# Layer 1 of a fused conv and state-space kernel: ACT scales the normalised tokens and sums the batch statistics, PE turns them back, DVE takes a second block of delta times x

## The chip, the cores and the metric

The kernel runs on one core of one Trainium2 chip. The metric is device time in microseconds (us) of one execution; the time before is the median of three runs. The engines are named as in the profile: PE (matmuls; PEld is its weight load), DVE (the vector engine), ACT (the scalar engine), POOL (GpSimd) and SP (the queue that issues the DMAs). Each engine works through its own instructions in the order in which the program emits them, and semaphores make it wait for the others.

## What is computed

The input x is 32 images of 96 channels, 56 x 56. Two stages follow each other. The first (an inverted bottleneck with squeeze and excitation) is not touched by the change. The second is, for each image, two state-space layers over the 3136 tokens, then a 1x1 convolution with a pooled branch, a batch normalisation over all images, and a residual:

```python
for i in range(2):                                     # seq: (32, 3136, 96)
    h = (seq - mean) * rsqrt(var + 1e-5) * ln_g + ln_b # over the 96 channels
    xs, z = split(h @ in_w)                            # 192 channels each
    xc = silu(causal_conv4(xs) + conv_b)
    dt, Bm, Cm = split(xc @ xproj_w)                   # 6, 16, 16
    delta = softplus(dt @ dt_w + dt_b)
    hs = scan(exp(delta * A), delta * Bm * xc)         # 192 channels x 16 states
    y = (sum over states of hs * Cm + Dp * xc) * silu(z)
    seq = seq + y @ out_w
out = fus_w @ concat(seq, relu(mean(x) @ gp_w + gp_b)) + fus_b
out = (out - mean(out)) * rsqrt(var(out) + 1e-5) * bn_g + bn_b + x   # over images and pixels
```

## The kernel before

Everything is float32. The first stage fills the first 3.5 ms or so and writes `x1d` to DRAM. The last 0.4 ms normalise `pred` and add the residual. The 15.2 ms in between are the two state-space layers.

**Units.** An image is cut into four chunks of 784 tokens (`LC`), and a chunk in one layer is a unit. There are 256 units; the list alternates a layer 0 unit of one chunk with a layer 1 unit of an older chunk. The state of the scan is carried from chunk to chunk in `state`.

**Steps.** A unit is 24 steps (`NT`), each a scan over 128 rows, 8 channels with 16 states. A block `k` of 64 channels takes 8 steps: 4 groups of states `j`, 2 halves `p`. One loop over `at` emits everything by hand. In step `at` it emits, in this order:

```python
inject(at + 4)   # POOL: bx = u * B, for the two halves at once         L851
decay(at + 1)    # ACT: da = exp(delta * A), into PSUM, two buffers     L831
bring(at)        # ACT: cp = copy of C into PSUM, one buffer, odd steps L839
early[at]        # the three Silu and Softplus, each with two table loads L587, L588
gated(at - 6); scan(at); product(at - 1)  # DVE: z *= y L914; scan L863; hc = hh * cp L871
save(at - 2); rest(at); reduce(at - 5)    # ACT L886; POOL hc L878; PE y L898, L903
todo[at]         # the rest, below; then the DMAs that fetch later steps
```

**The rest** is spread over steps by two lists. `prepare(n)` makes the inputs of unit n while the two units before it are scanned: its step t comes out in step t mod 24 of a unit. `finish(n)` projects the result one unit later. Within one step, `todo` holds the steps of the younger unit (small t) ahead of those of the older one (t over 23). What matters here, by step of the running unit:

- Steps 4 to 7, `finish`: PE makes the two halves `o` (L769, L773); ACT stores half 0 in step 6 and half 1 in step 7 (`seq` L779 for layer 0, `pre` L783 for layer 1, in the same buffer as `sq`). Step 19: DVE takes `bn_stats` of the two halves of a layer 1 unit (L788), and SP writes them to `pred`.
- Steps 23, 0, 1 and 2, younger unit: PE centers the tokens (`cen`), ACT copies the centered halves to `xm` (L618) and squares them (L619); the root follows.
- Steps 8 and 9: PE spreads the reciprocal roots over the channels, `rstd` (L656). Step 11: DVE multiplies both halves, `xn = xm * rstd` (L663).
- Step 12 and 13: PE runs the convolution of block 0, `xs`, from `xn` (`conv`, L675); step 14: ACT copies it to `xc` (`keep`, L686). Blocks 1 and 2 follow in steps 14 and 16, the copies in 16 and 18. Step 19 (early): Silu of `xc`.
- Step 11 (early), older unit: Softplus of `dl` on ACT, then `delta` is written to DRAM, and POOL makes blocks 1 and 2 of `us = dl * xc` (L725). Step 12: ACT copies block 0 of `xc` to PSUM (`up`, L730), DVE makes block 0 of `us` (L733), and SP writes `us` to DRAM in two DMAs; `fetch` reads it back for the next unit from step 16 on.

**Banks.** All these PE results, and `up`, take turns in two PSUM buffers: `bank()` (line 463) gives the n-th result the buffer of the n-2nd, so its first writer waits for that one's last reader.

Of the kernel before, what the change touches and what calls it, by code (L numbers as in the profile page):

```python
# [11 lines left out]
F32 = mybir.dt.float32  # L12
AF = mybir.ActivationFunctionType
ALU = mybir.AluOpType
AX = mybir.AxisListType
# [4 lines left out]
B, C, H, W = 32, 96, 56, 56  # L20
L = H * W
# [3 lines left out]
NL, NS, DIN, RANK, KC = 2, 16, 192, 6, 4  # L25
LC = 784
HB = LC // 2
LP = 512
NQ = L // LC
# [4 lines left out]
NB = DIN // 64  # L34
NT = 2 * NB * SG
TK = 112
NK = LC // TK
# [16 lines left out]
def conv_mamba_kernel(ctx, tc, a, out):  # L54
    nc = tc.nc
    v, s, g, pe, sp = nc.vector, nc.scalar, nc.gpsimd, nc.tensor, nc.sync

    const = ctx.enter_context(tc.tile_pool(name="const", bufs=1))
# [16 lines left out]
    gpw = load("gpw", [C, C])  # L75
    fusw = load("fusw", [C, 2, C])
    g2 = const.tile([C, B], F32, name="g2", tag="g2")
    stats = const.tile([C, B * NQ * 2, 6], F32, name="stats", tag="stats")

    def bn_fold(pool, gam, bet, mean, var, p, n, name):  # L80

# [13 lines left out]
    with ExitStack() as ph:  # L95
# [102 lines left out]
        for i in range(NHB):  # L198
            t = hp3.tile([128, H + 2, W + 2], F32, name=f"hpad{i}", tag=f"hpad{i}")
# [248 lines left out]
    with ExitStack() as ph:  # L448
# [5 lines left out]
        udram = ph.enter_context(tc.tile_pool(name="l1u", bufs=3, space=DRAM))  # L454
# [42 lines left out]
        ps = bank("acol")  # L497
# [16 lines left out]
        for i in range(NL):  # L514
            v.tensor_copy(lnb[:, i, C : C + 1], cp[:, LNB + i : LNB + i + 1])
            ps = bank(f"lnb_{i}")
# [43 lines left out]
        for k in range(NB):  # L560
            ps = bank(f"wf_{k}")
# [5 lines left out]
        state = [wts.tile([128, NT], F32, name=f"state{i}", tag=f"state{i}") for i in range(NL)]  # L567

        xn = wts.tile([C + 1, KC - 1 + LC], F32, name="xn", tag="xn")
# [4 lines left out]
        work = ph.enter_context(tc.tile_pool(name="l1", bufs=1))  # L574
        MAIN = "natural_log_exp_and_others"
        nch = B * NQ

        units = [(0, 0), (1, 0)]
        for c in range(2, nch):
# [3 lines left out]
        seqs = {}  # L583

        def through(t, func):

            s.activation(t, t, func)  # L587
            s.preload_act_table_set(MAIN)  # L588
# [3 lines left out]
        def cols(h):  # L592
            return slice(h * HB, h * HB + HB)

        def prepare(n):
# [5 lines left out]
            c, i = units[n]  # L601
            b, q = divmod(c, NQ)
            d = data[n]
# [9 lines left out]

            def square(h):
                if h == 0:
                    d["xm"] = wt([C, LC], "xm", 1, n)
                    d["sq"] = wt([C, LC], "sq", 1, n)
                s.copy(d["xm"][:, cols(h)], d["cen", h][:C, :HB])  # L618
                s.activation(d["sq"][:, cols(h)], d["cen", h][:C, :HB], AF.Square)  # L619

            def variance():
# [26 lines left out]
                    if q == 0:  # L648
                        g.memset(xn[:, : KC - 1], 0.0)

            def spread_root(h):
                ps = d["rstd", h] = bank(f"rstd_{n}_{h}")
                for k in range(NK):
                    lo, hi = max(k * TK, h * HB), min((k + 1) * TK, h * HB + HB)
                    if lo < hi:
                        pe.matmul(  # L656
                            ps[:C, lo - h * HB : hi - h * HB], d["rs"][:, k : k + 1].to_broadcast([TK, C]),
                            eye[:TK, lo - k * TK : hi - k * TK], start=True, stop=True,
                        )

            def normalise(h):
                to = xn[:C, KC - 1 + h * HB : KC - 1 + h * HB + HB]
                v.tensor_mul(to, d["xm"][:, cols(h)], d["rstd", h][:C, :HB])  # L663

            def trail():
                if q + 1 < NQ:
# [44 lines left out]
                for r in both:  # L711
                    pe.matmul(ps[r, :HB], wd[r, i, k, :], d["bcs"][r, :], start=True, stop=True)

            def spread(tag, t):
                to = d[tag] = udram.tile([DIN, LC], F32, name=f"{tag}d_{n}", tag=f"{tag}d")
                for h in range(2):
                    sp.dma_start(to[:, cols(h)].rearrange("(k m) l -> m k l", k=NB), t[h * 64 : h * 64 + 64])

            def softplus():
                through(d["dl"], AF.Softplus)  # L720
                spread("delta", d["dl"])

            def input_u():
                d["us"] = wt([128, NB, HB], "us", 1, n)
                g.tensor_mul(d["us"][:, 1:], d["dl"][:, 1:], d["xc"][:, 1:])  # L725

            def bring_x():

                d["up"] = bank(f"up_{n}")
                s.copy(d["up"][:, :HB], d["xc"][:, 0])  # L730

            def input_u0():
                v.tensor_mul(d["us"][:, 0], d["dl"][:, 0], d["up"][:, :HB])  # L733
                spread("u", d["us"])


            late, then = (9, 4) if n in (3, len(units) - 1) else (0, 0)
            steps = [(-4, load)]
# [1 line left out]
                steps += [(-1 + h + late, lambda h=h: center(h)), (-1 + 1 + h + late, lambda h=h: square(h))]  # L740
            steps += [(-1 + 2 + late, variance), (-1 + 3 + late, root), *[(t + late, lambda m=m: newton(m)) for m, t in enumerate((2, 2, 3))]]
            for h in range(2):
                steps += [(8 + h + then, lambda h=h: spread_root(h)), (11 + then, lambda h=h: normalise(h))]
            steps += [(11 + 3 + then, trail)]
            for k in range(NB):
                t = (12, 14, 16)[k] + then
# [3 lines left out]
            for k in range(NB):  # L750
                steps += [((17, 19, 21)[k] + then, lambda k=k: gate(k)), ((18, 20, 22)[k] + then, lambda k=k: keep("z", 3, "zp", k))]
                steps += [((22, 22, 23)[k] + then, lambda k=k: project_dt(k)), ((23, 23, 24)[k] + then, lambda k=k: keep("dl", 1, "dtp", k))]
            steps += [(26.5 + then, lambda: through(d["z"], AF.Silu)), (34.5 + then, softplus), (35 + then, input_u)]
            steps += [(36 + then, bring_x), (36 + then, input_u0)]
            return steps

        def finish(n):

            c, i = units[n]
            b, q = divmod(c, NQ)  # L760
            d = data[n]
# [12 lines left out]

            def store(h):
                if i + 1 < NL:
                    if h == 0:
                        seqs[c, i + 1] = wt([C, LC], f"seq{i + 1}", 3, n)
                    s.copy(seqs[c, i + 1][:, cols(h)], d["o", h][:C, :HB])  # L779
                    return  # L780
                if h == 0:
                    d["pre"] = wt([C, LC], "sq", 1, n)
                s.activation(d["pre"][:, cols(h)], d["o", h][:C, :HB], AF.Identity, bias=g2[:, b : b + 1])  # L783

            def count():
                if i + 1 == NL:
                    for h in range(2):
                        v.bn_stats(stats[:, 2 * c + h, :], d["pre"][:, cols(h)])  # L788
                    sp.dma_start(pred[b][:, q * LC : (q + 1) * LC], d["pre"])
                data[n] = {}  # L790

            return [
                (4, lambda: [project(k) for k in (None, 0, 1)]), (5, lambda: project(2)),
                (6, lambda: store(0)), (7, lambda: store(1)), (19, count),
            ]

        LAG = 5

        def place(t):
            k, r = divmod(t, 2 * SG)  # L800
            return k, r // 2, r % 2
# [76 lines left out]
                g.tensor_mul(hcs[at - 1][:, :, LP:], hhs[at - 1][:, :, LP:], beside(data[n]["C", j][:, LP:]))  # L878

        def save(at):  # L880
            n, t = divmod(at, NT)
            c, i = units[n]
            p = place(t)[2]
            hh = hhs[at - p] if p == 0 else hhs.pop(at - p)
            if c % NQ + 1 < NQ:
                s.copy(state[i][:, t : t + 1], hh[:, p, LC - 1 :])  # L886

        def reduce(at):

# [63 lines left out]
    with ExitStack() as ph:  # L953
        last = ph.enter_context(tc.tile_pool(name="last", bufs=3))
        one = ph.enter_context(tc.tile_pool(name="last1", bufs=1))
        mv = one.tile([C, 2], F32, name="mv", tag="mv")
        v.bn_aggr(mv, stats.rearrange("p n k -> p (n k)"))
        inv, sh = bn_fold(one, cp[:, BNG : BNG + 1], cp[:, BNB : BNB + 1], mv[:, 0:1], mv[:, 1:2], C, 1, "bn")
        for b in range(B):
            pre = last.tile([C, L], F32, name=f"lp{b}", tag="lp")  # L960
            res = last.tile([C, L], F32, name=f"lr{b}", tag="lr")
            sp.dma_start(pre, pred[b])
            sp.dma_start(res, x1d[b])
            s.activation(pre, pre, AF.Identity, bias=sh, scale=inv)
            v.tensor_add(res, res, pre)
            sp.dma_start(out[b], res)
# [61 lines left out]
```

## Time and profile before

| | |
|---|---|
| median of 3 runs | 19243.92 us (19236.5 to 19254.51) |
| the profiled execution | 19246.5 us, span 19243.6 us |
| the state-space layers, 3460 to 18700 us of the span | 15240 us, 59.5 us for each of 256 units |
| busy in that stretch: DVE, POOL, ACT, PE | 14955.52, 15124.08, 12552.34, 11335.55 us |
| mean granted clock of PE in that stretch | 0.79 of full speed |
| mean of one scan with a state, one `hc` on DVE, one `bx` on POOL, one `da` on ACT | 1835, 1194, 3573, 917 ns |

A line of the timeline gives the start from the beginning of the span, the duration, the engine, the line of the program, the operation with output and inputs, how many were merged, and in brackets how long the engine had been idle before it and what ended that. The duration of an instruction overlaps the start of the next one on its engine a little, so sums are better made from starts. The waits view gives, for each pair of waiting line and releasing line, the total in us, the times, and the longest.

### The profile page before, as it was taken

How to read it: one execution, taken by the hardware profiler on the slowest of the kernel's cores; microseconds unless marked ns; L12 is line 12 of the kernel's file. 1: busy time of each engine (PE TensorE's matmuls, PEld its weight loads, DVE VectorE, ACT ScalarE, POOL GpSimd, SP SyncE). 2: the span in 40 equal slices, each digit the busy share in tenths (PEclk: the TensorE clock that was granted, in tenths of full speed). 3: DMA queues.
4: the chain of work that ended last, by engine and by line, in shares of the span. 5: the costliest groups of instructions: out<-in, count | busy, mean ns of one | idle time of the engine just before them, and what ended most of it. 6: DMA issues, size and time to landing. Idle time of an engine off the chain costs nothing.

```text
span 19243.6 us, 282933 instructions
## 1 busy us (share of the span) xinstructions
PE 14489.7 (75%) x105692; PEld 5827.2 (30%) x105692; DVE 18041.5 (94%) x13684; ACT 14174.9 (74%) x23979; POOL 15509.9 (81%) x6606
## 2 busy tenths in 40 slices
PE   7999999677777777777777777777777777777760
PEld 3544444222222222222222222222222222222220
DVE  7888888699999999999999999999999999999993
ACT  3444444688888888888888888888888888888872
POOL 0000000699999999999999999999999999999991
PEclk9999999787777777877787778777877777778875
DMA  1000000355555555555555555555555555555548
GB/s 27 23 26 27 22 26 22 117 163 164 161 161 164 162 161 162 163 163 164 163 163 161 164 163 161 161 163 163 161 161 163 163 164 162 163 162 164 162 159 246
DMA packets 1049037, 2679.90 MB, mean 139 GB/s; under 512 B 129592, under 2 KB 342928, under 8 KB 1035368
## 3 DMA queue, kind: packets, MB, share of 16 engines
q1 hardware_dynamic: 1047656, 2661.80, 43.9%
q8 instruction: 828, 13.57, 0.3%
q14 instruction: 553, 4.53, 0.1%
HBM read 2211.05 MB, written 449.58 MB: 138 GB/s over the span
## 4 chain that ended last, share of the span: by engine, by line
DVE 35%; issue 24%; ACT 22%; PE 12%; POOL 4%; DMA 2%; SPq 1%; DVEq 0%; POOLq 0%; ACTq 0%
DVE hh L863 18%; DVE hc L871 12%; ACT da L831 5%; ACT L587 4%; ACT L588 3%; PE dw L276 3%; PE c L374 3%; POOL bx L851 2%; ACT cp L839 2%; DVE h L302 2%; DMA lr<-x1d 2%; PE bc L700 1%; PE c L223 1%; ACT dl L587 1%; ACT z L587 1%
## 5 line engine op out<-in xcount | busy, mean ns | idle before, releaser
L851 POOL TENSOR_TENSOR bx<-ub,B 128x1568 f32<-128x1568 f32 x3072 | 10975.8, 3573 | 25.2 <-DMA ub<-ud 15.8
L863 DVE TENSOR_TENSOR_SCAN hh<-da,state,bx 128x784 f32<-128x784 f32 x4608 | 8307.1, 1835 | 50.4 <-ACT da L831 44.8
L831 ACT ACTIVATE da<-deltab,acol 128x784 f32<-128x784 f32 x6144 | 5631.3, 917 | 2158.3 <-DVE hh L863 2124.2
L878 POOL TENSOR_TENSOR hc<-hh,C 128x544 f32<-128x544 f32 x3072 | 4210.3, 1371 | 40.2 <-DVE hh L863 28.8
L675 PE MATMUL xs<-xn,wx 97*64 97x392 f32 x12288 | 2907.0, 610 | 1356.5 <-DVE xn L663 1355.9
L871 DVE TENSOR_TENSOR hc<-hh,cp 128x1024 f32<-128x1024 f32 x3072 | 3667.7, 1194 | 0.1
L903 PE MATMUL y<-hc,rel 128*32 128x392 f32 x24576 | 3016.7, 579 | 367.7 <-DVE hc L871 349.2
L377 POOL TENSOR_TENSOR x<-x,x 96x784 f32<-96x784 f32 x128 | 276.5, 2160 | 3148.6 <-ACT x L376 3110.6
L863 DVE TENSOR_TENSOR_SCAN hh<-da,bx 128x784 f32<-128x784 f32 x1536 | 2679.1, 1774 | 53.4 <-ACT da L831 52.6
L675 PEld LDWEIGHTS xs<-xn,wx 97*64 97x64 f32 x12288 | 1307.8, 165 | 2982.0 <-DVE xn L663 1675.1
L302 DVE SCALAR_TENSOR_TENSOR h<-hpad,hp,h 128x1568 f32<-128x1568 f32 x1024 | 2036.3, 1989 | 34.3
L839 ACT COPY cp<-C 128x512 f32<-128x512 f32 x3072 | 1793.7, 584 | 371.6 <-DVE hc L871 369.2
L700 PE MATMUL bc<-xc,wbc 64*64 64x392 f32 x3072 | 975.5, 798 | 655.9 <-ACT xc L587 655.9
L903 PEld LDWEIGHTS y<-hc,rel 128*32 128x32 f32 x24576 | 579.8, 116 | 2092.5 <-issue 1155.1
L276 PE MATMUL dw<-hpad,diag 32*32 32x392 f32 x36864 | 1101.7, 515 | 38.6 <-issue 38.1
L691 PE MATMUL z<-xn,wz 97*64 97x392 f32 x3072 | 729.4, 555 | 480.4 <-ACT xc L686 462.3
L587 ACT ACT_TABLE_LOAD x768 | 985.3, 1283 | 13.8
L374 PE MATMUL c<-h,w3s 128*96 128x392 f32 (+1 forms) x2560 | 963.6, 521 | 40.3 <-DVE w3s L359 40.3
L588 ACT ACT_TABLE_LOAD x768 | 985.3, 1283 | 11.4
L223 PE MATMUL c<-x,w 96*128 96x392 f32 x2048 | 807.9, 551 | 193.1 <-DMA x<-in_x_dram 112.7
L283 ACT ACTIVATE h<-dw,tsh,tinv 128x392 f32<-128x392 f32 x512 | 340.0, 674 | 728.8 <-PE dw L276 728.8
L773 PE MATMUL o<-z,outw 64*96 64x392 f32 x3072 | 796.4, 652 | 97.4 <-DVE z L914 96.7
(156 smaller groups left out, 15639.9 us busy)
## 6 DMA issues: line engine op xcount, KB each, us to landing
deltab<-deltad SPq DMA_DIRECT2D x1536, 392.0 KB, 5.4
ub<-ud SPq DMA_DIRECT2D x1536, 392.0 KB, 5.8
B<-bcd SPq DMA_DIRECT2D x1024, 392.0 KB, 4.3
C<-bcd SPq DMA_DIRECT2D x1024, 392.0 KB, 4.2
deltad<-dl SPq DMA_DIRECT2D x512, 294.0 KB, 3.6
ud<-us SPq DMA_DIRECT2D x512, 294.0 KB, 3.6
x<-in_x_dram SPq DMA_DIRECT2D x32, 1176.0 KB, 7.4
x1d<-x SPq DMA_DIRECT2D x128, 294.0 KB, 2.6
```

Source lines behind the costliest of these rows:

```text
L276: pe.matmul(ps[r][to : to + 32, :HB], diag[src, n, t, :], hb[src, r0 : r0 + RB, dx : dx + W], start=t == 0, stop=t == 8, skip_group_check= ...
L302: v.scalar_tensor_tensor(acc, src, tap, acc, ALU.mult, ALU.add)
L587: s.activation(t, t, func)
L588: s.preload_act_table_set(MAIN)
L675: pe.matmul(d["xs", k][h * 64 : h * 64 + 64, :HB], wx[:, i, o, k * 64 : k * 64 + 64], xn[:, o + h * HB : o + h * HB + HB], start=o == 0, s ...
L831: s.activation(das[at][:, :LC], d["delta", k][:, p, :], AF.Exp, scale=acol[:, j, i, 2 * k + p : 2 * k + p + 1])
L839: s.copy(cps[at], data[n]["C", j][:, :LP])
L851: g.tensor_mul(bx, data[n]["u", k], beside(data[n]["B", j]))
L863: v.tensor_tensor_scan(hhs[at - p][:, p, :], das.pop(at)[:, :LC], bxs.pop(at), state[i][:, t : t + 1] if c % NQ else 0.0, ALU.mult, ALU.add,)
L871: v.tensor_mul(hcs[at - 1][:, :, :LP], hhs[at - 1][:, :, :LP], beside(cps.pop(at)))
L878: g.tensor_mul(hcs[at - 1][:, :, LP:], hhs[at - 1][:, :, LP:], beside(data[n]["C", j][:, LP:]))
L903: pe.matmul(yps[k][r0 : r0 + DB, :HB], rel, hc[:, p, h * HB : h * HB + HB], start=False, stop=j == SG - 1, skip_group_check=True,)
```

## The change

1. The normalisation moves from DVE to ACT and PE. `xm` and its two copies go. In steps 7 and 8 PE multiplies the tokens with the centering matrix so that the tokens lie on the partitions (`ct`, 4 and 3 blocks of 112 tokens); in steps 8 and 9 ACT scales the seven blocks by the reciprocal roots into `xt`; in steps 9 and 10 PE turns them back, `xn` in a bank; in steps 10 and 11 ACT copies the two halves into the tile `xn`. The spreading of the roots and the DVE product of step 11 go.
2. The batch statistics move from DVE to ACT. Each of the two `pre` activations also gives its sum, and a new Square about a pivot (the mean of the first half chunk) gives the sum of squares. `pre` gets a buffer of its own; it is written to `pred` in step 8 instead of 19. At the end a reduction and four small instructions replace `bn_aggr`.
3. Block 1 of `us` moves from POOL to DVE. ACT copies block 0 of `xc` in step 34 instead of 36 (step 10 of the running unit instead of 12) and block 1 in step 38 (14); DVE multiplies block 0 in step 36 (12) as before and block 1 in step 38 (14). `us` is written to DRAM in four DMAs instead of two.
4. `save` copies the states of two steps at once, every second step.

```diff
             def square(h):
                 if h == 0:
-                    d["xm"] = wt([C, LC], "xm", 1, n)
                     d["sq"] = wt([C, LC], "sq", 1, n)
-                s.copy(d["xm"][:, cols(h)], d["cen", h][:C, :HB])
                 s.activation(d["sq"][:, cols(h)], d["cen", h][:C, :HB], AF.Square)
...
-            def spread_root(h):
-                ps = d["rstd", h] = bank(f"rstd_{n}_{h}")
+            def turn(m):
+                ps = d["ct", m] = bank(f"ct_{n}_{m}")
+                for k in TURNS[m]:
+                    o = (k - TURNS[m][0]) * C
+                    pe.matmul(ps[:TK, o : o + C], seqs[c, i][:, k * TK : (k + 1) * TK], cen, start=True, stop=True)
+
+            def normalise(m):
+                if m == 0:
+                    d["xt"] = wt([TK, NK, C], "xt", 1, n)
+                for k in TURNS[m]:
+                    o = (k - TURNS[m][0]) * C
+                    s.activation(d["xt"][:, k, :], d["ct", m][:TK, o : o + C], AF.Copy, scale=d["rs"][:, k : k + 1])
+
+            def turn_back(h):
+                ps = d["xn", h] = bank(f"xn_{n}_{h}")
...
-                            ps[:C, lo - h * HB : hi - h * HB], d["rs"][:, k : k + 1].to_broadcast([TK, C]),
+                            ps[:C, lo - h * HB : hi - h * HB], d["xt"][:, k, :],
                             eye[:TK, lo - k * TK : hi - k * TK], start=True, stop=True,
...
-            def normalise(h):
+            def normal(h):
                 to = xn[:C, KC - 1 + h * HB : KC - 1 + h * HB + HB]
-                v.tensor_mul(to, d["xm"][:, cols(h)], d["rstd", h][:C, :HB])
+                s.copy(to, d["xn", h][:C, :HB])
...
-            def input_u():
-                d["us"] = wt([128, NB, HB], "us", 1, n)
-                g.tensor_mul(d["us"][:, 1:], d["dl"][:, 1:], d["xc"][:, 1:])
-
-            def bring_x():
-
-                d["up"] = bank(f"up_{n}")
-                s.copy(d["up"][:, :HB], d["xc"][:, 0])
-
-            def input_u0():
-                v.tensor_mul(d["us"][:, 0], d["dl"][:, 0], d["up"][:, :HB])
-                spread("u", d["us"])
+            def bring_x(k):
+
+                d["up", k] = bank(f"up_{n}_{k}")
+                s.copy(d["up", k][:, :HB], d["xc"][:, k])
+
+            def input_u(k):
+
+                if k == NB - 1:
+                    d["us"] = wt([128, NB, HB], "us", 1, n)
+                    g.tensor_mul(d["us"][:, k], d["dl"][:, k], d["xc"][:, k])
+                    return
+                v.tensor_mul(d["us"][:, k], d["dl"][:, k], d["up", k][:, :HB])
+                spread("u", d["us"], slice(0, 1) if k == 0 else slice(1, NB))
...
-                steps += [(8 + h + then, lambda h=h: spread_root(h)), (11 + then, lambda h=h: normalise(h))]
+                steps += [(7 + h + then, lambda h=h: turn(h)), (8 + h + then, lambda h=h: normalise(h))]
+                steps += [(9 + h + then, lambda h=h: turn_back(h)), (10 + h + then, lambda h=h: normal(h))]
...
-            steps += [(26.5 + then, lambda: through(d["z"], AF.Silu)), (34.5 + then, softplus), (35 + then, input_u)]
-            steps += [(36 + then, bring_x), (36 + then, input_u0)]
+            steps += [(26.5 + then, lambda: through(d["z"], AF.Silu)), (34.5 + then, softplus), (35 + then, lambda: input_u(NB - 1))]
+            steps += [(34 + then, lambda: bring_x(0)), (36 + then, lambda: input_u(0))]
+            steps += [(38 + then, lambda: bring_x(1)), (38 + then, lambda: input_u(1))]
...
-                    d["pre"] = wt([C, LC], "sq", 1, n)
-                s.activation(d["pre"][:, cols(h)], d["o", h][:C, :HB], AF.Identity, bias=g2[:, b : b + 1])
+                    d["pre"] = wt([C, LC], "pre", 1, n)
+                at = 2 * c + h
+                s.activation(
+                    d["pre"][:, cols(h)], d["o", h][:C, :HB], AF.Identity, bias=g2[:, b : b + 1],
+                    accum_out=stats[:, 0, at : at + 1],
+                )
+                if at == 0:
+                    s.activation(pivot, stats[:, 0, 0:1], AF.Copy, scale=-1.0 / HB)
+                squares = wt([C, HB], "squares", 1, at)
+                s.activation(squares, d["pre"][:, cols(h)], AF.Square, bias=pivot, accum_out=stats[:, 1, at : at + 1])
...
-                    for h in range(2):
-                        v.bn_stats(stats[:, 2 * c + h, :], d["pre"][:, cols(h)])
...
-                (6, lambda: store(0)), (7, lambda: store(1)), (19, count),
+                (6, lambda: store(0)), (7, lambda: store(1)), (8, count),
...
-            p = place(t)[2]
-            hh = hhs[at - p] if p == 0 else hhs.pop(at - p)
-            if c % NQ + 1 < NQ:
-                s.copy(state[i][:, t : t + 1], hh[:, p, LC - 1 :])
+            if place(t)[2] == 1:
+                hh = hhs.pop(at - 1)
+                if c % NQ + 1 < NQ:
+                    s.copy(state[i][:, t - 1 : t + 1], hh[:, :, LC - 1])
```

More of the change, by code (lines that the diff above doesn't have):

```diff
@@ L77, in conv_mamba_kernel @@
     g2 = const.tile([C, B], F32, name="g2", tag="g2")
-    stats = const.tile([C, B * NQ * 2, 6], F32, name="stats", tag="stats")
+    stats = const.tile([C, 2, B * NQ * 2], F32, name="stats", tag="stats")
+    pivot = const.tile([C, 1], F32, name="pivot", tag="pivot")
     def bn_fold(pool, gam, bet, mean, var, p, n, name):
@@ L576, in conv_mamba_kernel @@
         nch = B * NQ
+        TURNS = (range(NK - NK // 2), range(NK - NK // 2, NK))
         units = [(0, 0), (1, 0)]
@@ L712, in project_dt, with spread @@
                     pe.matmul(ps[r, :HB], wd[r, i, k, :], d["bcs"][r, :], start=True, stop=True)
-            def spread(tag, t):
-                to = d[tag] = udram.tile([DIN, LC], F32, name=f"{tag}d_{n}", tag=f"{tag}d")
+            def spread(tag, t, ks):
+                if tag not in d:
+                    d[tag] = udram.tile([DIN, LC], F32, name=f"{tag}d_{n}", tag=f"{tag}d")
                 for h in range(2):
-                    sp.dma_start(to[:, cols(h)].rearrange("(k m) l -> m k l", k=NB), t[h * 64 : h * 64 + 64])
+                    to = d[tag][:, cols(h)].rearrange("(k m) l -> m k l", k=NB)
+                    sp.dma_start(to[:, ks], t[h * 64 : h * 64 + 64, ks])
             def softplus():
                 through(d["dl"], AF.Softplus)
-                spread("delta", d["dl"])
-            def input_u():
-                d["us"] = wt([128, NB, HB], "us", 1, n)
-                g.tensor_mul(d["us"][:, 1:], d["dl"][:, 1:], d["xc"][:, 1:])
-            def bring_x():
-                d["up"] = bank(f"up_{n}")
-                s.copy(d["up"][:, :HB], d["xc"][:, 0])
-            def input_u0():
-                v.tensor_mul(d["us"][:, 0], d["dl"][:, 0], d["up"][:, :HB])
-                spread("u", d["us"])
+                spread("delta", d["dl"], slice(0, NB))
+            def bring_x(k):
[8 more added lines that the diff above has]
+                spread("u", d["us"], slice(0, 1) if k == 0 else slice(1, NB))
             late, then = (9, 4) if n in (3, len(units) - 1) else (0, 0)
@@ L956, in conv_mamba_kernel @@
         mv = one.tile([C, 2], F32, name="mv", tag="mv")
-        v.bn_aggr(mv, stats.rearrange("p n k -> p (n k)"))
+        off = one.tile([C, 1], F32, name="off", tag="off")
+        v.tensor_reduce(mv, stats, AX.X, ALU.add)
+        v.tensor_scalar(mv, mv, 1.0 / (B * L), None, ALU.mult)
+        v.tensor_add(off, mv[:, 0:1], pivot)
+        v.tensor_mul(off, off, off)
+        v.tensor_sub(mv[:, 1:2], mv[:, 1:2], off)
         inv, sh = bn_fold(one, cp[:, BNG : BNG + 1], cp[:, BNB : BNB + 1], mv[:, 0:1], mv[:, 1:2], C, 1, "bn")
```

## The prediction

> **What bounds the kernel now.** I read the page first, then the busy times of the state-space stretch, the waits inside it, the timeline of some units, and PE's granted clock around one wait. The stretch holds 15240 of 19244 us, and of its engines two are full (columns: length, then PE, PEld, DVE, ACT, POOL busy):
>
> ```profile
> 3460.00:18700.00 15240.00, 11335.55 (x61716) 4176.15 (x61716) 14955.52 (x11708) 12552.34 (x21527) 15124.08 (x6418) 0.79 0.51 162
> ```
>
> POOL is busy 99.2% and DVE 98.1%. Who waits for whom decides between them:
>
> ```profile
> PE xs L675 <- DVE xn L663: 1355.9, 254, 6.0
> ...
> DVE us L733 <- ACT up L730: 109.8, 256, 5.0
> ...
> DVE hh L863 <- ACT da L831: 97.4, 215, 19.0
> ...
> POOL hc L878 <- DVE hh L863: 25.5, 54, 2.9
> ```
>
> The first line, PE waiting over 5 us in every unit for `xn`, costs nothing today, but will matter below. DVE hardly ever waits for POOL (0.8 us in all); POOL waits for DVE's scans now and then. So DVE sets the pace at 59.53 us a unit, POOL follows with 59.4 to 59.5 of its own, and DVE's only idle time, about 1 us a unit, is for ACT: once for `up` in every unit, and for a `da` behind a table load. The next view is the timeline of steps 11 to 15 of a unit that scans layer 1 (I call it A; a unit that scans layer 0, and in which a layer 1 unit is finished, is B):
>
> ```profile
> 11029.76 1.28 ACT L587 ACT_TABLE_LOAD   x1
> 11030.79 1.00 DVE L663 TENSOR_TENSOR xn<-xm,rstd 96x392 f32<-96x392 f32 x2
> ...
> 11031.38 5.96 PE L675 MATMUL xs<-xn,wx 97*64 97x392 f32 x16 [5.29 <-DVE xn L663]
> ...
> 11032.25 1.28 ACT L588 ACT_TABLE_LOAD   x1
> ...
> 11033.64 0.91 ACT L831 ACTIVATE da<-deltab,acol 128x784 f32<-128x784 f32 x1
> ...
> 11034.58 0.48 ACT L730 COPY up<-xc 128x392 f32<-128x392 f32 x1
> ...
> 11035.09 0.56 DVE L733 TENSOR_TENSOR us<-dl,up 128x392 f32<-128x392 f32 x1 [0.42 <-ACT up L730]
> ...
> 11036.04 3.58 DVE L863 TENSOR_TENSOR_SCAN hh<-da,state,bx 128x784 f32<-128x784 f32 x2
> ...
> 11038.95 0.47 ACT L686 COPY xc<-xs 128x392 f32<-128x392 f32 x1
> ...
> 11039.54 1.20 DVE L871 TENSOR_TENSOR hc<-hh,cp 128x1024 f32<-128x1024 f32 x1
> ...
> 11040.65 1.84 DVE L863 TENSOR_TENSOR_SCAN hh<-da,state,bx 128x784 f32<-128x784 f32 x1
> ```
>
> ACT is in Softplus with its two table loads from 29.76 to 33.53 (I leave out the 11000 from here on). Meanwhile DVE makes `xn`, and PE starts the convolution of block 0 at 31.38. It takes 5.96 us here; the 16 matmuls of a later block take 2.86. The windows of 2 us show why (the eighth number is the granted clock):
>
> ```profile
> 11032.00:11034.00 2.00, 2.00 (x8) 1.27 (x8) 2.00 (x2) 1.97 (x4) 2.00 (x2) 0.50 0.21 49
> ...
> 11036.00:11038.00 2.00, 2.00 (x9) 0.35 (x5) 2.00 (x3) 0.63 (x3) 2.00 (x1) 0.50 0.56 121
> 11038.00:11040.00 2.00, 2.00 (x18) 0.55 (x16) 2.00 (x2) 1.76 (x5) 2.00 (x3) 0.98 0.77 210
> ```
>
> After 5.29 us of idling PE runs at half clock for some 6 us. Over 240 units of the timeline that first convolution takes 4.80 to 5.97 us, 5.59 in the mean.
>
> **POOL and DVE, counted alone.** POOL's product shrinks from 784 to 392 columns. Rows of 544 and 784 columns (1371 and 1876 ns) give 2.1 ns a column, so 1.05 us: POOL loses 0.83 us a unit and needs 58.65. DVE loses the two products of step 11, 0.93 us from start to start, and in every B the two `bn_stats`, 0.93; it gains one product of 0.48 (35.09 to the next start at 35.57). If nothing waited, that were 0.92 us a unit. But the moved work lands on ACT and PE, and DVE waits on ACT already.
>
> **ACT before Softplus, steps 6 to 11.** A scaled block of 112 x 96: `va`, 112 x 7 with a column operand, takes 264 ns, and `dl`, 392 columns with one, 580; that is 0.82 ns a column and 337 ns for 96. Back to back ACT saves about 0.1 (two copies of 0.47 start 0.38 apart at 48.08), so 0.24 each, 1.7 us for seven; without that overlap 2.4. Add a copy of 0.40 and `up` of 0.42; take off four state copies of 0.09. That makes 2.2 us. In A, ACT idles 0.33, 0.67, 0.71, 1.05 and 0.71 us before the `da` of these steps, 3.5 in all: it fits. In B each `pre` (0.58) gains an accumulator read and a Square with another: in the first stage an activation with a sum starts 0.66 after the one before, so about 1.37 a half, 1.6 us more in all, 3.8 against idle times of 0.17, 0.50, 0.65, 0.99, 0.65 and two of 0.19 plus 0.3 of overlap: it just fits. Price 0; without the overlap Softplus comes 0.31 (A) and 0.54 us (B) late. The new PE work of these steps, seven turning matmuls beside as many back as before, falls where PE waits for ACT's stores anyway.
>
> **The step that moves behind Softplus.** The second `normal` is emitted in step 11, Softplus in the early list of step 11. So ACT copies the second half of `xn` only after 33.53: a state copy at 33.55, `normal` at 33.64, done at 34.12. The bank of `xs` is the one that this copy reads, so all of the convolution waits for it: from 34.18 instead of 31.38. PE's last work before that, the turning back (ready to start at 26.3) and the `y` of step 12, ends by 29.6, so it idles 4.6 us; the trace has an idle time of 2.85 us, at 50.3, after which the clock is at 0.50. So I take the mean 5.59, bounds 4.80 and 5.97. It ends at 39.77. In step 14 ACT copies that result to `xc` ahead of the new `up` of block 1, since the younger unit's steps come first: `xc` at 39.82, `up` at 40.22 to 40.70. Queued behind the waiting `xc` on ACT is this `up`, and DVE waits for it with scan 15 and everything else behind: block 1 of `us` at 40.73, scan 15 at 41.21. It was 40.65. Without that wait DVE would be there earlier: `da` of step 13 goes behind `normal`, 34.04 to 34.96, scan 13 at 34.99, `hc` 3.50 later, `us` 1.11 after it, scan 15 at 40.08. So the 1.43 us that DVE saves up to here (0.93, and 0.50 between `hc` and the product that waited for `up`) are spent on 0.48 of new product, 0.38 of waiting at scan 13 (DVE is ready at 34.61) and 1.13 at `up`: +0.56 us.
>
> At one point the Trainium skill stands against the row that this rests on. "TensorE: Matmul & The Clock Gate", Part 1, says that PE gets its full clock after about 3.4 us of sustained work. By that the convolution would take 3.4 and half of the remaining 2.56, 4.68 us, scan 15 would come at 40.30, and the sum below would end 134 us under the time before. The windows above show half clock until 38, over 6 us after the start, so I go by the row.
>
> **The second cover.** In B the removed `bn_stats` hid most of a wait for another table load:
>
> ```profile
> 11110.48 1.01 DVE L788 BATCH_NORM_STATS2 stats<-sq 96x6 f32<-96x392 f32 x2
> ...
> 11113.39 0.91 ACT L831 ACTIVATE da<-deltab,acol 128x784 f32<-128x784 f32 x1
> ...
> 11114.68 3.46 DVE L863 TENSOR_TENSOR_SCAN hh<-da,bx 128x784 f32<-128x784 f32 x2
> ```
>
> `da` ends at 114.30, behind the Silu of `xc`; the scan starts at 114.68. With 0.93 taken out ahead of it, the scan moves by no more than 0.38, less 0.03 of signal: 0.35. (A, which has no `bn_stats`, waits 0.39 there today.)
>
> **Sum.** A: +0.56. B: +0.56 - 0.35 = +0.21. Mean 0.385, times 256 units: +99 us. Nothing elsewhere: the last reduction is hidden behind the loads of `lr`; halving the state copies takes 0.09 off ACT where it idles; SP has two more DMAs of 0.6 us, and its fetches queue behind the wait for block 1 of `us`, about 3 us later than now, but its `ub` then lands at 52.5 where POOL's `bx` needs it at 54.3; `pred` written in step 8 holds SP's fetches for step 16 until 81, and POOL needs them at 94. The profiled execution took 19246.5 us (span 19243.6), 2.6 over the median; from the median the sum is 19343 us.
>
> **The rivals.**
> - *The relief holds (faster).* If the convolution takes no more than 4.46 us and so ends by 38.64, `up` is ready when DVE arrives at 39.60. Then A gains 0.57 and B 0.92, 0.745 in the mean, 191 us: 19053. POOL's 58.65 would allow it. For it: ACT has some 10 us of idle time a unit, and PE is busier before this convolution, which may find a better clock. Against: PE idles 4.6 us in front of it, and no unit of the trace was under 4.80.
> - *ACT is crowded (slower still).* If ACT's small scalings don't overlap, Softplus comes 0.31 and 0.54 late and everything behind it, mean 0.43, another 109 us: 19452. It decides once the work added in steps 6 to 11 passes the 3.5 us of idle time.
> - *The DMA is late (slower).* If the read of block 0 waits for the whole of `us`, it starts at about 45.5 instead of 40.3; it costs only if `us` slips 1.8 us more, then up to 0.5 us a unit: 19470.
>
> **How the numbers follow.** 0.2%, 38 us or 0.15 us a unit, is about what a measurement of this kernel can tell from no change. The forecast's mechanism has 0.53: with the convolution between 4.80 and 5.97 us A lies between -0.23 and +0.94, so B at -0.58 to +0.59, 19140 to 19440; of it 0.39 slower, 0.10 same, 0.04 faster. Relief 0.24, faster. Crowding 0.17, of it 0.02 same, where a quicker convolution makes up for it. DMA 0.06, of it 0.01 same. That makes faster 0.28, same 0.13, slower 0.59. The forecast's own range is 19140 to 19440; the range of 8 in 10 takes in a good part of the relief at the low end and of the crowding at the high end: 19070 to 19450.
>
> **What would show it.** Right: a wait of DVE for `up` of about 1.1 us in each unit, at the second `us` and not the first; ACT waiting for PE `xs` in each unit; the first convolution starting about 0.6 us after Softplus ends; POOL waiting for DVE's scans much more often, since it is 0.8 us a unit faster. Wrong: no such wait at the second `us`, or an `xs` of 3 to 4 us; Softplus starting late after an ACT without idle time; POOL waiting for `ub`.

## The result, and the profile after

The changed kernel takes 19347.47 us (median of 4 runs, 19343.66 to 19366.23); the kernel before, on the same chip, 19249.21 us (19236.5 to 19269.49). The ratio is 1.0053, 95% interval 1.0037 to 1.0069: the change costs some 98 us, and the forecast was 99. The profiled execution after has a span of 19344.5 us.

The state-space stretch first, with the columns of the prediction's first fence (length, PE, PEld, DVE, ACT, POOL busy, granted clock):

```profile
3460.00:18800.00 15340.00, 11938.36 (x65324) 4422.55 (x65326) 14750.58 (x11214) 13048.59 (x22026) 14942.57 (x6417) 0.81 0.49 161
```

DVE is busy 96.2% (98.1% before) and POOL 97.4% (99.2%): both lost the work that the change takes from them, and neither is full any more. ACT gained some 500 us. The waits of this stretch name what came in between:

```profile
PE xs L690 <- DVE us L751: 1248.7, 253, 6.6
ACT xc L701 <- PE xs L690: 593.0, 421, 4.8
DVE us L751 <- ACT up L743: 258.8, 253, 7.3
POOL hc L904 <- DVE hh L889: 250.1, 365, 6.3
DVE hh L889 <- ACT da L857: 213.7, 573, 1.4
```

The third line is the one that was forecast: DVE waits for `up` once a unit, 1.02 us each time (before 0.43). ACT's wait for PE's `xs` is as good as new (second line; 593 us in all, 20.3 before). POOL waits for DVE's scans ten times as long as before, so DVE with its waits sets the pace, not POOL. And DVE waits for `da` more than twice as long. The timeline of a unit that scans layer 0 (a B) shows the chain, from the second table load of Softplus to scan 15:

```profile
11034.25 1.28 ACT L591 ACT_TABLE_LOAD   x1
11035.55 0.48 ACT L678 COPY xn<-xn 96x392 f32<-96x392 f32 x1
11035.65 0.56 DVE L751 TENSOR_TENSOR us<-dl,up 128x392 f32<-128x392 f32 x1
...
11036.26 5.25 PE L690 MATMUL xs<-xn,wx 97*64 97x392 f32 x16 [6.57 <-DVE us L751]
11036.88 3.59 DVE L889 TENSOR_TENSOR_SCAN hh<-da,state,bx 128x784 f32<-128x784 f32 x2 [0.20 <-ACT da L857]
...
11041.57 0.48 ACT L701 COPY xc<-xs 128x392 f32<-128x392 f32 x1 [1.77 <-PE xs L690]
11042.08 0.49 ACT L743 COPY up<-xc 128x392 f32<-128x392 f32 x1
...
11042.60 0.56 DVE L751 TENSOR_TENSOR us<-dl,up 128x392 f32<-128x392 f32 x1 [1.02 <-ACT up L743]
11043.08 3.58 DVE L889 TENSOR_TENSOR_SCAN hh<-da,state,bx 128x784 f32<-128x784 f32 x2
```

The second half of the new copy of `xn` (L678) sits behind Softplus on ACT; the convolution of block 0 starts only behind it and the first `us` (which of the two holds it is told below, under the bank) and takes 5.25 us; ACT waits 1.77 us to copy it out, makes `up` of block 1 behind that, and DVE idles 1.02 us until it is there. The first `us` (L751 at 35.65) does not wait: its `up` was copied ahead of Softplus. PE's clock during the convolution (eighth number):

```profile
11036.26:11039.00 2.74, 2.74 (x10) 1.07 (x12) 2.54 (x3) 2.17 (x4) 2.74 (x1) 0.50 0.91 240
11039.00:11041.00 2.00, 2.00 (x10) 0.64 (x6) 2.00 (x2) 0.80 (x2) 2.00 (x3) 0.50 0.00 0
11041.00:11043.00 2.00, 2.00 (x16) 0.35 (x12) 0.98 (x2) 1.40 (x3) 2.00 (x1) 0.96 0.00 0
```

It stays at half until about 11041, some 4.8 us after the start, nearly the whole convolution.

Means over units 10 to 250, from the trace, with S the end of Softplus's second table load:

| us | before A / B | forecast A / B | after A / B |
|---|---|---|---|
| unit | 59.39 / 59.80 | +0.56 / +0.21 | 59.96 / 59.85 (+0.56 / +0.05 before rounding) |
| start of the first convolution, from S | -2.17 | +0.65 | +0.69 |
| its length | 5.59 | 5.59 | 5.34 / 5.26 |
| wait at the second `us` | none made | 1.13 | 1.03 / 0.95 |
| scan 15, from S | 7.04 | 7.68 | 7.60 / 7.52 |
| wait for `da` at scan 21 | 0.40 / 0 | 0.39 / 0.58 | 0.48 / 0.47 |

The 0.58 is what the prediction's own terms leave in B: 0.93 less, of which 0.35 is gained.

### The profile page after: what moved, and what is told of

Read it like the earlier page. It is cut to its first block, busy times and chain, and to the rows that moved or that the text cites. A ratio compares the mean times of both kernels' runs of the same rounds, so it can differ in the third digit from the quotient of the medians.

```text
span 19344.5 us, 291519 instructions
## 1 busy us (share of the span) xinstructions
PE 15105.1 (78%) x109276; PEld 6080.2 (31%) x109276; DVE 17829.6 (92%) x13176; ACT 14677.5 (76%) x24492; POOL 15331.8 (79%) x6606
## 4 chain that ended last, share of the span: by engine, by line
issue 38%; DVE 27%; ACT 16%; PE 13%; POOL 2%; DMA 2%; SPq 1%; DVEq 0%; POOLq 0%; ACTq 0%
DVE hc L897 13%; DVE hh L889 10%; PE xs L690 8%; ACT da L857 3%; ACT L590 3%; DVE h L304 2%; ACT cp L865 2%; ACT L591 2%; DMA lr<-x1d 2%; ACT xc L590 1%; PE bc L715 1%; POOL bx L877 1%; ACT z L590 1%; DVE us L751 1%; PE y L930 1%
## 5 line engine op out<-in xcount | busy, mean ns | idle before, releaser
L904 POOL TENSOR_TENSOR hc<-hh,C 128x544 f32<-128x544 f32 x3072 | 4143.8, 1349 | 295.3 <-DVE hh L889 254.7
L690 PE MATMUL xs<-xn,wx 97*64 97x392 f32 x12288 | 2827.1, 613 | 1248.7 <-DVE us L751 1248.7
L930 PE MATMUL y<-hc,rel 128*32 128x392 f32 x24576 | 2946.7, 561 | 29.0 <-DVE hc L897 18.3
L690 PEld LDWEIGHTS xs<-xn,wx 97*64 97x64 f32 x12288 | 995.8, 165 | 3045.2 <-DVE us L751 1497.5
L671 PE MATMUL xn<-eye,xt 112*96 112x112 f32 (+1 forms) x4096 | 768.6, 358 | 420.7 <-ACT xt L664 420.0
L930 PEld LDWEIGHTS y<-hc,rel 128*32 128x32 f32 x24576 | 537.4, 113 | 1443.9 <-issue 1233.1
L793 PE MATMUL o<-z,outw 64*96 64x392 f32 x3072 | 912.4, 732 | 81.2 <-DVE z L941 80.4
```

Of the source, the lines that this page charges most:

```text
L690: pe.matmul(d["xs", k][h * 64 : h * 64 + 64, :HB], wx[:, i, o, k * 64 : k * 64 + 64], xn[:, o + h * HB : o + h * HB + HB], start=o == 0, s ...
L930: pe.matmul(yps[k][r0 : r0 + DB, :HB], rel, hc[:, p, h * HB : h * HB + HB], start=False, stop=j == SG - 1, skip_group_check=True,)
```

## The experiments

Theory: the second `normal`, behind Softplus, delays the convolution; the convolution is long because PE has idled and its clock has fallen; `up` of block 1 is queued behind the result; DVE waits for it. The rivals: POOL or the DMA sets the pace, ACT is crowded, or part 2 or 3 by itself costs the time. Ratios are to the kernel before on the same chip, with 95% intervals. "Units" below is the mean over units 10 to 250 of each profile, 59.60 us before and 59.90 after.

**The second `up` earlier.** The kernel after, where `up` of block 1 no longer stands behind the waiting `xc`:

```diff
-            steps += [(38 + then, lambda: bring_x(1)), (38 + then, lambda: input_u(1))]
+            steps += [(36 + then, lambda: bring_x(1)), (38 + then, lambda: input_u(1))]
```

> The changed kernel with one step moved: the copy of block 1 of xc to PSUM (up) comes out in step 12 of the running unit instead of 14, ahead of the copy that waits for the convolution on PE; the DVE product stays in step 14. Theory (the wait of DVE for this copy, about 1 us a unit, is the cost): the wait at the second us is gone, scan 15 comes 1.0 us earlier. Behind it ACT still waits for the late convolution, so part of it may come back at the Silu of xc; 90 to 270 us under the changed kernel, 19080 to 19260 us. Rival (ACT is simply crowded by the added work): the same work in another place, 19350 us within 30.

Measured: 19195.63 us (7 runs), ratio 0.9972 (0.9961 to 0.9983), inside the range. Its waits in the stretch:

```profile
ACT xc L701 <- PE xs L690: 932.0, 665, 4.5
DVE hh L889 <- ACT da L857: 358.5, 609, 19.0
DVE us L751 <- ACT up L743: 1.8, 1, 1.8
```

DVE's wait for `up` is gone (1.8 us once), although the convolution still starts 0.69 us after S and still takes 5.26. Scan 15 comes 6.48 us after S, 1.1 earlier, but the unit gains only 0.60 (59.31): ACT still waits for the late convolution (932 us now), so `xc`, its Silu and the `da` behind that come late, and DVE waits 0.83 to 0.89 us at scan 21. So the late convolution is paid for twice: at the second `us`, and, where that is relieved, at scan 21.

**The second `normal` earlier.** The kernel after, with that copy ahead of Softplus:

```diff
-                steps += [(9 + h + then, lambda h=h: turn_back(h)), (10 + h + then, lambda h=h: normal(h))]
+                steps += [(9 + h + then, lambda h=h: turn_back(h)), (10 + h / 2 + then, lambda h=h: normal(h))]
```

> The changed kernel with one step moved: the second copy into xn comes out ahead of Softplus in step 11 instead of behind it; in the program the first convolution then shares its bank with that copy and no longer with up. Theory: the convolution starts about 4 us earlier relative to the end of Softplus, ACT finds it done, up is in time, and DVE waits for neither; Softplus comes 0.4 us later and still scan 15 comes 1.0 us earlier; 19080 us, POOL's own 58.7 us a unit close behind. Rival (ACT is crowded): Softplus 0.4 us later, so 100 us slower, 19450 us.

Measured: 19061.02 us (4 runs, 19060.26 to 19066.64), ratio 0.9903 (0.9886 to 0.9919): half a step of order on one 0.48 us copy, with the bank that changes by it, is worth 286 us, and this version beats both kernels. Its waits:

```profile
PE xs L690 <- ACT xn L678: 228.3, 213, 2.5
...
DVE hh L889 <- ACT da L857: 203.6, 576, 2.8
...
ACT xc L701 <- PE xs L690: 15.7, 7, 3.5
POOL hc L904 <- DVE hh L889: 13.3, 9, 4.3
...
DVE us L751 <- ACT up L743: 6.1, 2, 3.5
```

The convolution starts 3.74 us before S and takes 3.68 in the mean; DVE no longer waits behind it, and ACT waits for PE's `xs` 7 times in all. Two things changed at once, as the expectation says: the first convolution now waits for the copy of `xn` (first line), and no longer for the first `us`, which in the kernel after ends only 0.64 us after S. With the old bank the convolution could not have started so early, so the 286 us are the price of both together. POOL waits for DVE 9 times in all, so POOL is the bound, at 58.75 us a unit; the prediction counted 58.65 for it.

**PE kept busy ahead of the convolution.** Everything of the kernel after stays in its order; PE only repeats the turning back of the second half (same operands, same bank) in step 11, five times, or three:

```diff
+            def again():
+                ps = d["xn", 1]
+                for r in range(5):
+                    for k in range(NK):
...
+            steps += [(11 + then, again)]
```

> The kernel after, with the turning back of the second half (turn_back(1)) done five times more in step 11, after the first one and ahead of the y of step 12: the same matmuls into the same bank, the same values. They only fill PE's idle time of 4.8 to 5.1 us ahead of the first convolution, at about 0.96 us each; the convolution still cannot start before 0.69 us after Softplus. Theory (the convolution is long because PE has idled before it, and its length is what DVE waits for at the second us): it takes 3 to 4 us instead of 5.3 in most units, DVE's wait for up (1.0 us a unit, 258.8 us in all) falls under 60 us, a unit becomes 59.2 to 59.4 us as with the earlier up, and the time 19200 us (19150 to 19270). Rival 1 (the convolution is slow for another reason, its operands or what runs beside it): it stays at 5.3 us, the wait stays, 19350 us. Rival 2 (PE's extra work is itself in the way: the y of step 12, behind it, holds up DVE's product with z ahead of scan 13): the wait moves to that product, 19350 us or more.

> The same with three repetitions, so that about 2 us of idle time stay ahead of the convolution. Theory: idle times of 1.5 to 2.5 us stood ahead of convolutions of 2.86 to 5.96 us in the earlier profiles, so some units gain and some do not; convolution 4 to 5 us in the mean, wait 80 to 200 us, time 19230 to 19310. If only the start of the convolution mattered and not its length: 19350. If any matmul work ahead is enough: 19200, as with five.

Measured: 19100.38 us with five (4 runs, ratio 0.9919, 0.9904 to 0.9934) and 19117.82 with three (4 runs, 0.9929, 0.9913 to 0.9946). Both lie under the ranges expected, by 50 and 112 us, and under the kernel before: useless matmuls save 247 us of the kernel after. With three the convolution takes 3.69 us in the mean and DVE waits 67.6 us for `up` in all, less than the 4 to 5 and the 80 to 200 expected; the intervals of the two runs overlap, so they are not told apart. The timeline with five, of a unit that scans layer 0, and the clock around its first convolution:

```profile
11063.58 4.59 PE L682 MATMUL xn<-eye,xt 112*96 112x56 f32 x40
...
11068.40 0.48 ACT L689 COPY xn<-xn 96x392 f32<-96x392 f32 x1
...
11068.90 2.87 PE L701 MATMUL xs<-xn,wx 97*64 97x392 f32 x16
...
11074.22 0.56 DVE L762 TENSOR_TENSOR us<-dl,up 128x392 f32<-128x392 f32 x1
```

```profile
11067.00:11069.00 2.00, 2.00 (x23) 1.24 (x23) 1.83 (x3) 1.99 (x4) 2.00 (x3) 1.00 0.34 73
11069.00:11072.00 3.00, 3.00 (x18) 1.28 (x20) 2.84 (x3) 2.62 (x5) 3.00 (x2) 1.00 0.85 222
```

The convolution starts where it started (0.73 and 0.84 us after S in B and A), but at a granted clock of 1.00 at its start, and takes 2.86 us in B and 3.71 in A. The second `us` waits 0.00 and 0.13, and scan 21 only 0.40: with the convolution short, both payments fall away, where the earlier `up` had saved the first alone. That is the part that the expectation, taken from that run, missed (59.31 there, 58.88 here). The rival that PE's work is itself in the way shows up as well, small: DVE's `z` waits for the delayed `y` 128 times, 57.5 us in all.

**More convolution.** Two matmuls in front of block 0's convolution, into its bank (the same lines in the kernel before, for the second run):

```diff
+                for h in range(2) if (k, taps[0]) == (0, 0) else ():
+                    pe.matmul(
+                        d["xs", k][h * 64 : h * 64 + 64, :HB], wx[:, i, 0, :64], xn[:, h * HB : h * HB + HB],
+                        start=True, stop=True,
+                    )
```

> The changed kernel with two more matmuls (of the form of the others) ahead of the first convolution of block 0, into the same bank; the output stays the same. At half clock two take 1.3 to 1.5 us. Theory (this convolution lies on the path, through the copy to xc and up to DVE): 1.3 us more a unit, 19670 to 19730 us. Rival (ACT is crowded, PE has room): within 30 us of the changed kernel.

> The kernel before with the same two more matmuls ahead of the first convolution. Theory: here the convolution starts 2.2 us before Softplus ends and has 2 us to spare before ACT copies it: within 30 us of the kernel before. Rival (any work on PE between normalisation and xc costs time): as much as in the changed kernel, some 270 us slower.

Measured: in the kernel after 19619.51 us (4 runs, ratio 1.0192, 1.0177 to 1.0208), so 272 us more; in the kernel before 19247.18 (10 runs, 0.9997, 0.9988 to 1.0007), nothing. The same work is free before, where the convolution starts 2.17 us before S, and fully paid after, at the wait that was named:

```profile
DVE us L756 <- ACT up L748: 527.9, 249, 8.0
```

That is 2.12 us each, 1.1 more than in the kernel after. The expectation had 1.3 to 1.5, which was too much; the two matmuls and the convolution together last 6.41 us, 1.11 more than 5.30.

**Part 1 alone, in the kernel before** (the normalisation on ACT and PE; the root's spreading and `xm` go):

```diff
-                steps += [(8 + h + then, lambda h=h: spread_root(h)), (11 + then, lambda h=h: normalise(h))]
+                steps += [(7 + h + then, lambda h=h: turn(h)), (8 + h + then, lambda h=h: normalise(h))]
+                steps += [(9 + h + then, lambda h=h: turn_back(h)), (10 + h + then, lambda h=h: normal(h))]
```

> The kernel before with part 1 of the change alone (the normalisation by ACT and PE); statistics, us and the state copies as before. Theory: DVE loses 0.93 us of products a unit but waits for up in step 12, which now stands behind the second copy into xn: scan 13 comes 0.4 us later after Softplus than before, none of the relief is left; 0.4 us a unit slower than before, 19350 us. Rival (the relief holds where no second product follows): 0.5 to 0.9 us a unit faster, 19020 to 19120 us.

Measured: 19369.70 us (4 runs), ratio 1.0061 (1.0046 to 1.0076), 20 over the figure expected; units 60.02. Here the one `up` of step 12 stands behind `normal`, which stands behind Softplus:

```profile
DVE us L746 <- ACT up L743: 448.5, 255, 11.4
```

1.76 us each against 0.43: part 1 alone loses about as much as the whole change (the intervals of 1.0061 and 1.0053 overlap), through the same copy but at another wait.

**Parts 2 and 4 alone, in the kernel before** (statistics on ACT, states saved two at a time):

```diff
-                    for h in range(2):
-                        v.bn_stats(stats[:, 2 * c + h, :], d["pre"][:, cols(h)])
...
+                s.activation(squares, d["pre"][:, cols(h)], AF.Square, bias=pivot, accum_out=stats[:, 1, at : at + 1])
```

> The kernel before with parts 2 and 4 alone (statistics on ACT, the state copies halved); normalisation and us as before. Theory: only every second unit had bn_stats, and they hid most of a wait for the da behind the Silu of xc, so 0.35 to 0.46 us of 0.93 is left, in every second unit, 45 to 60 us in all; POOL's own 59.47 us a unit, now the longer one, takes some of it: 25 to 50 us faster than before. Rival (DVE's time counts in full): 0.93 in every second unit, 119 us faster. Rival (ACT is crowded by the squares and sums): slower than before.

Measured: 19219.67 us (10 runs), ratio 0.9981 (0.9972 to 0.9991), 33 us faster, as expected. Of DVE's 0.93 us in B 0.31 are left: B takes 59.49 us, and A is about as long as before (59.44). Both limits that the expectation named are in the trace: the wait for `da` at scan 21 of B is 0.25 us (none before), and DVE waits for POOL's `bx` 154 times, 51.5 us in all (0.8 us before). How the rest divides is not shown.

**Part 3 undone, in the kernel after** (blocks 1 and 2 of `us` on POOL again, one `up` in step 12):

```diff
-            steps += [(34 + then, lambda: bring_x(0)), (36 + then, lambda: input_u(0))]
-            steps += [(38 + then, lambda: bring_x(1)), (38 + then, lambda: input_u(1))]
+            steps += [(36 + then, bring_x), (36 + then, input_u0)]
```

> The changed kernel with part 3 undone: blocks 1 and 2 of us on POOL, one product on DVE, up in step 12, as before; parts 1, 2 and 4 stay. Theory: without a second product there is no second wait, but the wait for the one up grows as in the run with part 1 alone (0.42 us a unit more than before), less the 0.2 of the statistics: 0.2 us a unit slower than before, 50 us, so about 50 us faster than the changed kernel. Rival (part 3 is the whole loss): 100 to 200 us faster than before.

Measured: 19299.34 us (10 runs), ratio 1.0023 (1.0013 to 1.0032), 47 over the kernel before, as expected; units 59.73. So parts 1, 2 and 4 make 47 of the loss, and part 3 on top of them makes the other half, some 50. Part 3 by itself was not run.

**The kernel before once more**, for what lies ahead of the first scan:

> The kernel before once more, for a second profile: in the changed kernel and four others the first scan starts 21 to 37 us later than in the one profile of before, though no line of the first stage differs. If that is spread from run to run, this profile has its first scan at 3555 to 3575 us; if the kernels differ there, at 3541 within 5.

Measured: 19231.92 us, span 19229.7; the first scan starts at 3536.0 us, at 3540.9 in the first profile of that kernel and at 3566.3 in the kernel after. In the other profiles it starts at 3558 to 3577, and once at 3600.3 (five repetitions). By the bounds that the expectation set, 3536.0 speaks for a difference between the programs. But one of the others is the kernel before with the two matmuls, whose first stage is the same line for line: 3560.6. So this part varies by 20 to 25 us without any difference in its lines. Whether the two low values of the kernel before are chance or go with that program is open.

This second profile also has the means of A and B: 59.30 and 59.79 us, against 59.39 and 59.80 in the first. The difference in A is mostly four units of the first profile that take 61.88 or 61.89 us, where the second has 59.64 or 59.65 for the same units.

## Why the prediction was right, and where its steps were off

**The mechanism stood.** Each sign named ahead is in the trace: the wait at the second `us` and not the first, ACT waiting for `xs`, the convolution about 0.6 us after Softplus, POOL waiting for DVE ten times as long. Six runs show that it is the cause, and does not merely stand there: move the copy, move `up`, or shorten the convolution without moving anything, and the loss goes; lengthen the convolution, and the loss grows after and not before.

**The clock.** The prediction took the row (half clock for over 6 us behind an idle PE) against a rule. The Trainium skill, "TensorE: Matmul & The Clock Gate", Part 1, gives about 3.4 us of sustained work until the full clock. Here half clock lasted some 4.8 us in the unit shown, and the convolution took 5.30 in the mean and never under 4.70, so the estimate of 4.68 by the rule lies under every one of 240 units. That a busy PE keeps its clock is what the repeated matmuls show.

One reading of the prediction says more than its row: "after 5.29 us of idling PE runs at half clock". In that unit PE was at half clock already while it still worked, ahead of the idle time (the kernel before, eighth number):

```profile
11022.00:11024.00 2.00, 2.00 (x13) 0.73 (x11) 2.00 (x2) 1.29 (x3) 2.00 (x3) 0.50 0.89 331
```

So the kernel before did not show by itself that the idle time is the reason. The runs with repeated matmuls do, for the kernel after.

**A: +0.56, in part by luck.** Scan 15 moved from 7.04 to 7.60 us after S, +0.56 as forecast, but several terms of that sum were off and cancel: the convolution was 0.25 shorter than taken, its start 0.04 later, from its end to that of `up` 1.05 us instead of 0.93 (39.77 to 40.70), and the unit that the forecast started from had scan 15 at 7.12, a little later than the mean of 7.04. Behind scan 15 the forecast left the wait for `da` as it was, and it grew by 0.08. That does not show in the total mostly because the four long units lift the mean of A before; against the second profile A is 0.66 longer.

**B: +0.05 against +0.21.** The step "the scan moves by no more than 0.38, less 0.03" took the lead of `da` from one unit. Over 120 B units before the mean lead is 0.49 and 0.38 is the smallest, so 0.46 could be gained. Scan 15 is later by 0.47, Softplus 0.05 earlier in the unit, and `da` for scan 21 falls back another 0.08 against scan 15: that makes +0.04, and +0.05 was measured. A term that is paid 128 times wants the mean, and one row of the timeline gives only a sample.

**The sum.** By units it should have been 0.31 x 256 = 78 us, and over the 240 units it is 14376.4 - 14303.2 = 73. Against the second profile of the kernel before it is 0.36 x 256, some 91. The rest of the loss lies ahead of the first scan, in lines that the change does not touch: 25 us later than in the first profile, 30 than in the second. So the agreement of 98 with 99 is better than the steps were: they were some 10 to 20 us too high, and a difference outside their scope filled it up.

**The bank.** The text ahead of the prediction and the prediction say that the n-th result takes the buffer of the n-2nd, and that `xs` therefore waits for the bank that the second `normal` reads. The trace puts PE's wait down to DVE's first `us`: in the program as built, `xs` of block 0 got the bank of `up`. So the rule of the n-2nd does not hold here. It made no difference to the sum, because the first `us` ends 0.64 us after S and `normal` 0.56. With part 3 undone, `xs` does not wait for `us`, and its first matmuls, on the first half of the tokens, start 4 us before S.

**The rivals.** The relief was priced at 19053, on the condition that the convolution takes no more than 4.46 us. Where that was brought about in the mean, by the repeated matmuls, the time was 19100 with five and 19118 with three; with the copy moved it was 19061. ACT is not crowded: Softplus ends 31.22 us into a unit, 31.24 to 31.29 in the two profiles before. The prediction's "it just fits" for B was not shown by its own numbers (3.64 us of idle time against 3.8), but the trace bears it out. The DMA is not late: POOL's `bx` waits for `ub` 4 times in the whole stretch.

## What to carry to other kernels

When an operation moves from one engine to another, look at what stands ahead of it in the new engine's queue, not at how long it takes: a 0.48 us copy behind a table load cost more than the whole relief brought, and with it ahead, and the bank that came with that, the same change gained 189 us. Where a later wait depends on PE, count PE's idle time in front of it as part of the price, because the clock that it meets can nearly double the length (5.30 us against 2.86 here). A term that is paid in every unit is taken as a mean over the units.

## What was not expected of the hardware

How much idle time PE stands without losing its clock showed up in the two runs with repeated matmuls, over 480 units: with under 1.5 us of idle time ahead of it, the first convolution took 2.86 to 2.88 us in all 273 units; with 1.5 to 2.5 us it took 4.55 in each of 60 units of one kernel, and 2.97 in the mean in 51 units of the other; with more, 3.92 to 5.50. The last idle time is not all that counts, however: in the version with the copy ahead of Softplus, convolutions of 5.50 us occur after less than 0.5 us of idle time, and in the run with parts 2 and 4 alone 25 convolutions behind 1.5 to 2.5 us took 5.64 to 5.97.

What they have in common is in the clock record of the traces. In the version with the copy ahead, the 154 convolutions that start at a granted clock of 1.00 take 2.88 us in the mean, and the 86 that start at 0.50 take 5.10; in the kernels before and after all 240 start at 0.50. What lowered the clock ahead of those 86 stays open. In that record the granted clock changes only at whole multiples of 3.41 us after the change before (over 1600 changes in each of six traces: before, after and four of the versions), so it can also fall during a convolution: the 60 of 4.55 us all start at 1.00.

Two more matmuls at the head of the slow convolution cost 1.11 us after and, in the kernel before, 0.76 (6.35 against 5.59). By the 2.86 us of 16 matmuls at the full clock, two would be an estimated 0.36.
